# Second cross-attention layer and feed-forward in one stage: a group's feed-forward in 25 steps, one in each half step of later groups' attention

## The chip, the cores and the metric

The kernel runs on one core of a Trainium2 chip. A core has five engines that run beside each other, each with its own instruction stream: TensorE (PE; its weight loads are listed as PEld), VectorE (DVE), ScalarE (ACT), GpSimd (POOL) and SyncE (SP, which here issues nearly all DMA transfers). The metric is device time in microseconds, the median of several runs.

## The reference

The reference is a decoder of two layers over x of 64 sequences x 128 rows x 256 features, each with three pre-normalized parts. The change touches the last two parts of the second layer. Cut to them:

```python
x = x + xattn(layernorm(x), ctx)       # 16 heads of 16 features
x = x + ffn(layernorm(x))

def xattn(y, c):
    q, k, v = (y @ Wq.T + bq) * 0.25, c @ Wk.T + bk, c @ Wv.T + bv     # then split in heads
    return merge_heads(softmax(q @ k.T) @ v) @ Wo.T + bo

def act_quant(x):
    scale = 127.0 / clip(max(abs(x), axis=-1), 1e-5)
    return clip(round(x * scale), -128, 127) / scale

def bit_linear(x, w):                  # weight_quant: ternary weights, one scale
    return act_quant(x) @ weight_quant(w).T

def ffn(x):
    h = bit_linear(x, w1)              # 256 -> 1024
    h = silu(depthwise_conv1d(h, conv_w, 3 taps along the 128 rows) + conv_b)
    return bit_linear(h, w2)           # 1024 -> 256
```

## The kernel before, in words

The work is cut into 16 groups of GB = 4 sequences. The kernel is a row of stages: window attention, cross attention of layer 0 with its slot feed-forward mixed in, causal attention of layer 1 (`stage_attn` with cross False), cross attention of layer 1 (`stage_attn` with cross True), and the feed-forward of layer 1 (`stage_bitnet`). Each stage runs over all groups and hands x on through DRAM: `Flow.reach` loads a group into one of eight SBUF tiles, `Flow.store` and `Flow.flush` write it out (`ab`, `cd`, `de`, `ef`, `out`). The order within an engine is set when the program is built, from the order in which the Python code issues instructions and from estimates of when their inputs are ready; the trace shows such moves, for instance the tap matrices of the last stage (L1156) made on POOL from 2244.6 us, before cross attention began. Waits are put in by the same tool from what each instruction reads and writes.

PSUM has eight banks. Four are the small tiles of `psum(k)` (name `ps`); the other four are one score tile (`sc`) in attention, and four single tiles (`cv`) in the feed-forward.

`attention_stage` works on one sequence at a time in two half steps, for eight heads each. In half step j, `score_burst` (L444) computes scores of sequence j // 2 in the layout that gives a row maximum and, for the sequence one and a half earlier, the transposed scores with the maximum already taken off, 16 and 16 small matmuls into the one score tile. `score_halves` then takes the exponential of the second half on ScalarE (L467; with a bias L464 and L465) and the negated row maximum of the first on VectorE (`negmax`, L471). Even half steps then run `shift_query` (L482, L486) and `divide` (L506 to L513), odd ones `weigh_values` (L494, L499), `turn_output` (L523, L525) and `finish_batch` (L176). At the end of each half step `tick(j)` is called; in `stage_attn` it advances `group_project`, the normalization and projections of the next group (L143, L155, L167, L1046, L1057, L1062, and the addition of the output bias to x on POOL, L1025), which is a generator cut into a few parts.

`stage_bitnet` runs 18 iterations of nine steps, over three groups at once: one group's hidden blocks and convolutions, the scales and rounding of the group before, the output of the one before that. `bitnet_in` normalizes and quantizes x (L1178 to L1192), transposes it (L1198) and spreads the scales over rows (`bcast_rows`, L1166, L1168). `bitnet_hidden` is a bf16 projection (L167) and the scaling into a padded tile `hp` (L1212). `bitnet_conv` does the three taps in one of two ways: for the blocks in `CONV_PE` as three matmuls with diagonal matrices (L1222) and Silu with the bias on ScalarE as eviction (L1226), for the others with one ScalarE step (L1231), two VectorE steps (L1235, L1238) and Silu (L1241). Abs and maxima follow (L1337, L1338), `bitnet_scale` (L1247 to L1268), `bitnet_quant`: the product on POOL (L1276) and rounding on VectorE (L1277), and `bitnet_out` (L1284, L1288).

Of the kernel before, what the change touches and what calls it, by code (L numbers as in the profile page):

```python
# [10 lines left out]
F = mybir.dt.float32  # L11
BF = mybir.dt.bfloat16
# [14 lines left out]
CONV_PE = (0, 1, 3, 4, 6)  # L27
# [978 lines left out]
def stage_attn(k, w, cross, bias=None):  # L1006
    nc = k.nc
    pre = "we" if cross else "wd"
    bias_t, bias_s = bias if bias is not None else (None, None)
    with k.tc.tile_pool(name=pre, bufs=2) as wp, k.tc.tile_pool(name=pre + "1", bufs=1) as w1:  # L1010
        vas = []
        for i in range(2):
            va = w1.tile([S, GB, H, 32], F, name=f"{pre}va{i}")
            nc.gpsimd.memset(va, 0.0)
            nc.gpsimd.memset(va[:, :, :, 16:17], 1.0)
            vas.append(va)
        proj, pending = {}, {}

        def group_project(g):

            xn = w1.tile([S, GB, D], F, tag="xn", name="xn")
            cx = load_group(k, w1, g) if cross else None
# [8 lines left out]
            if cross:  # L1031
                kvT = w1.tile([128, 2, GB * S], F, tag="kvT", name="kvT")
                transpose_group(k, cx, kvT)
            else:
                kvT = xnT
# [3 lines left out]
            for dst, wt, src, sc, bi in (  # L1039
                (qt, w.wq, xnT, w.parq, w.bq), (kt, w.wk, kvT, w.par, w.bk)  # L1040
            ):
                for cc in range(2):
                    p = psum(k)
                    project(k, p, wt, cc * 128, 128, src, 0, GB * S)
                    for par in range(2):
                        nc.scalar.activation(  # L1046
                            dst[:, 2 * cc + par], p, AF.Identity,
                            scale=sc[:, par : par + 1], bias=bi[:, cc, par : par + 1],
                        )
                    yield  # L1050
            va = vas[g % 2]
            for b2 in range(2):
                p = psum(k)
                for j in range(2):
                    b = b2 * 2 + j
                    for kc in range(2):
                        nc.tensor.matmul(  # L1057
                            p[:, j * D : (j + 1) * D], kvT[:, kc, b * S : (b + 1) * S],
                            w.wv[:, kc, :], start=(kc == 0), stop=(kc == 1),
                        )  # L1060
                for j in range(2):
                    nc.vector.tensor_tensor(  # L1062
                        va[:, b2 * 2 + j, :, 0:DH],
                        p[:, j * D : (j + 1) * D].rearrange("p (h d) -> p h d", d=DH),
                        w.bv.rearrange("p (h d) -> p h d", d=DH), ALU.add,
                    )
                if b2 == 0:
                    yield
# [103 lines left out]
def bitnet_in(k, w, g, wp, done):  # L1172
    nc = k.nc
    k.flow.reach(g + 1)
    xn = wp.tile([S, GB, D], F, tag="xn", name="xn")
# [4 lines left out]
    sc = wp.tile([S, GB], F, tag="sc", name="scl")  # L1180
# [10 lines left out]
    xq = wp.tile([S, GB, D], BF, tag="xq", name="xq")  # L1191
# [11 lines left out]
    p = bcast_rows(k, wp, cl, "dg")  # L1203
    isb = wp.tile([128, GB, S], F, tag="isb", name="isb")
    nc.scalar.copy(isb, p.rearrange("p (b l) -> p b l", l=S))
    done.append((xqT, isb))


def bitnet_hidden(k, w, j, xqT, isb, hp):
    p = psum(k)  # L1210
    project(k, p, w.w1, j * 128, 128, xqT, 0, GB * S)
    k.nc.vector.tensor_tensor(  # L1212
        hp[:, :, 1 : S + 1], p.rearrange("p (b l) -> p b l", l=S), isb, ALU.mult
    )


def bitnet_conv(k, w, j, hs, hp):
    nc = k.nc
    if j in CONV_PE:
        pc = k.sc.tile([128, GB, S], F, tag="cv", name="cv")  # L1220
        for t in range(3):
            nc.tensor.matmul(  # L1222
                pc, w.taps[:, CONV_PE.index(j), t, :], hp[:, :, t : t + S],
                start=(t == 0), stop=(t == 2),
            )
        nc.scalar.activation(  # L1226
            hs[:, j, :], pc.rearrange("p b l -> p (b l)"), AF.Silu, bias=w.cb[:, j : j + 1]
        )
        return
    hj = hs[:, j, :].rearrange("p (b l) -> p b l", l=S)  # L1230
    nc.scalar.activation(  # L1231
        hj, hp[:, :, 1 : S + 1], AF.Identity, scale=w.cw[:, j, 1:2],
        bias=w.cb[:, j : j + 1],
    )
    nc.vector.scalar_tensor_tensor(  # L1235
        hj, hp[:, :, 0:S], w.cw[:, j, 0:1], hj, ALU.mult, ALU.add
    )
    nc.vector.scalar_tensor_tensor(  # L1238
        hj, hp[:, :, 2 : S + 2], w.cw[:, j, 2:3], hj, ALU.mult, ALU.add
    )  # L1240
    nc.scalar.activation(hj, hj, AF.Silu)  # L1241


def bitnet_scale(k, w, m4, wp, done):

    nc = k.nc
    nc.vector.tensor_tensor(m4[:, 0:2], m4[:, 0:2], m4[:, 2:4], ALU.max)  # L1247
    mx = wp.tile([128, GB * S], F, tag="mx", name="mx")
    nc.vector.tensor_tensor(mx, m4[:, 0], m4[:, 1], ALU.max)
    p = psum(k)  # L1250
    for b in range(GB):
        nc.tensor.transpose(
            p[:, b * S : (b + 1) * S], mx[:, b * S : (b + 1) * S], k.ident
        )
    yield
    c2 = wp.tile([S, GB], F, tag="c2", name="c2")
# [9 lines left out]
    p = bcast_rows(k, wp, s2, "dg")  # L1266
    s2b = wp.tile([128, GB * S], F, tag="s2b", name="s2b")
    nc.scalar.copy(s2b, p)  # L1268
    done.append((c2, s2b))


def bitnet_quant(k, j, hs, s2b, uq):


    nc = k.nc
    nc.gpsimd.tensor_tensor(hs[:, j], hs[:, j], s2b, ALU.mult)  # L1276
    nc.vector.tensor_scalar(uq[:, j], hs[:, j], MAGIC, MAGIC, ALU.add, ALU.subtract)  # L1277


def bitnet_out(k, w, g, b, uq, c2):  # L1280
    nc = k.nc
    p = psum(k)
    for j in range(8):
        nc.tensor.matmul(  # L1284
            p[:, 0:D], uq[:, j, b * S : (b + 1) * S], w.w2[:, j, :],
            start=(j == 0), stop=(j == 7),
        )
    nc.vector.scalar_tensor_tensor(  # L1288
        k.x[g][:, b, :], p[:, 0:D], c2[:, b : b + 1], k.x[g][:, b, :],
        ALU.mult, ALU.add,  # L1290
    )
    if b == GB - 1:
        k.flow.store(g)


QUANT_AT = {3: (0,), 4: (1, 2), 5: (3,), 6: (4, 5), 7: (6,), 8: (7,)}


def stage_bitnet(k, w):

    nc = k.nc
    with k.tc.tile_pool(name="wf", bufs=2) as wp, k.tc.tile_pool(name="wf1", bufs=1) as w1:
        hps = []
        tap_matrices(k, w, w1)
        for i in range(4):
            hp = w1.tile([128, GB, S + 2], F, name=f"hp{i}")
            nc.gpsimd.memset(hp, 0.0)
            hps.append(hp)  # L1310
        n = 0
        k.flow.reach(0)
        inputs = []
        for _ in bitnet_in(k, w, 0, wp, inputs):
            pass
        scaled = out = None
        for g in range(k.G + 2):
            hs = None
            if g < k.G:
                xqT, isb = inputs.pop()  # L1320
                hs = wp.tile([128, 8, GB * S], F, tag="hs", name="hs")
                m4 = wp.tile([128, 4, GB * S], F, tag="m4", name="m4")
# [195 lines left out]
```

## Time and profile before

| | us |
|---|---|
| median of 3 runs (3495.82 to 3513.59) | 3497.22 |
| the profiled execution | 3494.91 |
| its span, first to last instruction | 3493.1 |
| PE busy in the span | 2893.9 (83%) |
| DVE busy | 2568.4 (74%) |
| ACT busy | 1311.4 (38%) |
| POOL busy | 998.4 (29%) |
| mean granted TensorE clock | 0.910 |

Busy time is the time in which an engine had an instruction running. The span holds all five stages; cross attention of layer 1 begins near 2249 us, with the last matmul of causal attention, and the feed-forward's first matmul starts at 2880.42 us. In rows of groups, the columns are: line, engine, operation, output <- inputs with their shapes, count | busy us, mean ns of one | idle time of the engine just before, and what ended it. The granted clock is a share of TensorE's full speed.

### The profile page before, as it was taken

The page shows a single profiled execution, that of the slowest core. Times are in us where ns is not written, and L with a number is a line of the kernel's source. Part 1 is how long each engine was busy: PE and PEld are TensorE (multiplying, and loading weights), DVE is VectorE, ACT ScalarE, POOL GpSimd, SP SyncE. Part 2 cuts the span into 40 slices and gives each one's busy share as a digit, 9 for nine tenths or more (in the row PEclk, how much of TensorE's full clock was granted, in tenths as well). Part 3 has the DMA queues.
Part 4 walks back from the last instruction along what each step waited for, and adds up shares of the span by engine and source line. Part 5 has one row for each costly group of instructions (what it writes and reads, how often), then busy time and mean ns, then how long its engine had stood idle before and what let it go on. Part 6 is the DMA issues. An engine that isn't in the chain of part 4 may idle for free.

```text
span 3493.1 us, 65076 instructions
## 1 busy us (share of the span) xinstructions
PE 2893.9 (83%) x27764; PEld 1845.9 (53%) x27764; DVE 2568.4 (74%) x4875; ACT 1311.4 (38%) x2012; POOL 998.4 (29%) x920
## 2 busy tenths in 40 slices
PE   5868888588888888878999999699999977777776
PEld 2433333366666666645666666466766753333332
DVE  6867786566666666658989889766665559888876
ACT  1121111144444444424444444244445534444442
POOL 6446555343333433220000000210010003334323
PEclk9869999699999999979999999899999998888887
DMA  4100100101011010000000000101111110001000
GB/s 143 61 13 25 37 31 31 49 14 38 20 37 38 19 38 26 13 37 13 26 26 25 26 26 26 49 32 38 38 56 38 48 40 12 24 24 37 13 13 24
DMA packets 59249, 115.20 MB, mean 33 GB/s; under 512 B 6496, under 2 KB 39664, under 8 KB 58704
## 3 DMA queue, kind: packets, MB, share of 16 engines
q1 hardware_dynamic: 58304, 109.29, 8.9%
q8 instruction: 219, 3.59, 0.4%
q0 software_dynamic: 656, 1.75, 0.2%
q14 instruction: 70, 0.57, 0.1%
HBM read 69.08 MB, written 41.94 MB: 32 GB/s over the span
## 4 chain that ended last, share of the span: by engine, by line
PE 41%; DVE 37%; POOL 9%; ACT 7%; issue 4%; DMA 1%; SPq 0%; POOLq 0%; DVEq 0%; ACTq 0%
PE sc L444 10%; PE ps L167 7%; DVE negmax L471 6%; PE ps L176 5%; PE ps L494 4%; DVE uq L1277 4%; DVE sb L458 3%; DVE e L464 3%; PE cv L1222 2%; DVE xn L143 2%; DVE pv L350 2%; ACT e L465 2%; DVE oT L354 2%; PE ps L482 2%; PE ps L1057 2%
## 5 line engine op out<-in xcount | busy, mean ns | idle before, releaser
L444 PE MATMUL sc<-kt,qt 32*128 32x128 f32 x6144 | 517.7, 296 | 150.8 <-DVE negmax L471 93.0
L444 PEld LDWEIGHTS sc<-kt,qt 32*128 32x128 f32 x6144 | 422.9, 195 | 330.0 <-issue 151.0
L444 PE MATMUL sc<-q,kt 32*128 32x128 f32 x6144 | 490.6, 295 | 5.6 <-DVE q L486 3.0
L471 DVE TENSOR_REDUCE negmax<-sc 128x8 f32<-128x1024 f32 x256 | 312.4, 1220 | 159.7 <-ACT e L467 154.5
L444 PEld LDWEIGHTS sc<-q,kt 32*128 32x128 f32 x6144 | 406.3, 195 | 25.7 <-DVE rec L509 11.4
L467 ACT ACTIVATE e<-sc 128x1024 f32<-128x1024 f32 x256 | 261.5, 1021 | 296.8 <-PE sc L444 296.5
L1222 PE MATMUL cv<-hp,taps 128*128 128x512 f32 x480 | 263.3, 692 | 60.5 <-DVE hp L1212 59.8
L292 POOL TENSOR_TENSOR pr<-pad,qt 128x896 f32<-128x896 f32 x128 | 244.9, 1947 | 188.9 <-ACT pad L279 180.8
L486 DVE TENSOR_TENSOR q<-ps,qt 128x512 f32<-128x512 f32 x192 | 131.7, 686 | 154.3 <-PE ps L482 154.3
L1276 POOL TENSOR_TENSOR hs<-hs,s2b 128x512 f32<-128x512 f32 x128 | 177.2, 1418 | 194.7 <-ACT s2b L1268 194.7
L465 ACT ACTIVATE e<-e 128x1024 f32<-128x1024 f32 x128 | 135.3, 1057 | 241.7 <-DVE e L464 241.7
L458 DVE TENSOR_TENSOR sb<-sc,bias_s 128x1024 f32<-128x1024 f32 x128 | 156.2, 1220 | 69.4 <-PE sc L444 69.4
L1222 PEld LDWEIGHTS cv<-hp,taps 128*128 128x128 f32 x480 | 98.2, 215 | 192.3 <-issue 95.0
L350 DVE TENSOR_TENSOR pv<-sc,pad 128x896 f32<-128x896 f32 x128 | 136.9, 1082 | 73.4 <-PE sc L344 73.3
L136 POOL TENSOR_TENSOR ln_rs<-ln_ve,expo 128x4 f32<-128x4 f32 x96 | 101.2, 1054 | 304.0 <-DVE ln_ve L135 166.4
L1025 POOL TENSOR_TENSOR x<-x,t_d_bo 128x1024 f32<-128x1024 f32 x16 | 37.6, 2351 | 490.5 <-DVE xn L143 490.5
L499 ACT COPY avs<-ps 128x512 f32<-128x512 f32 x192 | 112.2, 584 | 149.1 <-PE ps L494 149.1
L1025 POOL TENSOR_TENSOR x<-x,t_e_bo 128x1024 f32<-128x1024 f32 x16 | 37.5, 2344 | 443.1 <-DVE xn L143 443.1
L464 DVE TENSOR_TENSOR e<-sc,bias_t 128x1024 f32<-128x1024 f32 x128 | 155.4, 1214 | 1.6 <-PE sc L444 1.3
L471 DVE TENSOR_REDUCE negmax<-sb 128x8 f32<-128x1024 f32 x128 | 154.8, 1210 | 0.0
L133 DVE BATCH_NORM_STATS2 ln_st<-x 128x6 f32<-128x256 f32 x384 | 152.2, 426 | 2.6 <-DMA x<-cd 0.6
L1277 DVE TENSOR_SCALAR uq<-hs 128x512 bf16<-128x512 f32 x128 | 146.4, 1191 | 7.3 <-POOL hs L1276 7.3
(329 smaller groups left out, 6450.4 us busy)
## 6 DMA issues: line engine op xcount, KB each, us to landing
cx<-in_ctx_dram SPq DMA_DIRECT2D x32, 512.0 KB, 4.1
x<-in_x_dram SPq DMA_DIRECT2D x16, 512.0 KB, 3.9
ab<-x SPq DMA_DIRECT2D x16, 512.0 KB, 2.6
x<-ab SPq DMA_DIRECT2D x16, 512.0 KB, 3.2
cd<-x SPq DMA_DIRECT2D x16, 512.0 KB, 2.6
x<-cd SPq DMA_DIRECT2D x16, 512.0 KB, 3.2
de<-x SPq DMA_DIRECT2D x16, 512.0 KB, 2.6
x<-de SPq DMA_DIRECT2D x16, 512.0 KB, 3.2
```

The source lines that it names most:

```text
L167: k.nc.tensor.matmul(out, w[:, kc, c0 : c0 + cn], rhsT[:, kc, n0 : n0 + n], start=(kc == 0), stop=(kc == 1),)
L292: k.nc.gpsimd.tensor_tensor(pr[:, c], shift_windows(t.kt, b, c), t.qt[:, c, b, :].unsqueeze(1).to_broadcast([128, WIN, S]), ALU.mult,)
L350: nc.vector.tensor_tensor(pv, bc[th][:, :, 0 : WIN * 64].rearrange("p c (l w) -> p c l w", w=WIN), shift_windows2(t.vt, b, th), ALU.mult,)
L444: k.nc.tensor.matmul(t[:, side * 2 + rr, c * S : (c + 1) * S], st[rows, c, :], mv[rows, c, :], start=True, stop=True,)
L458: nc.vector.tensor_tensor(sb, src, bias_s[:, hf * 2 : hf * 2 + 2, :], ALU.add)
L464: nc.vector.tensor_tensor(e, t[:, 2:4, :], bias_t[:, hf * 2 : hf * 2 + 2, :], ALU.add)
L465: nc.scalar.activation(e, e, AF.Exp)
L467: nc.scalar.activation(e, t[:, 2:4, :], AF.Exp)
L471: nc.vector.tensor_reduce(b.lay.extra(b.nm, hf * 2), src.rearrange("p r (c m) -> p r c m", m=S), AX.X, ALU.max, negate=True,)
L1222: nc.tensor.matmul(pc, w.taps[:, CONV_PE.index(j), t, :], hp[:, :, t : t + S], start=(t == 0), stop=(t == 2),)
L1276: nc.gpsimd.tensor_tensor(hs[:, j], hs[:, j], s2b, ALU.mult)
L1277: nc.vector.tensor_scalar(uq[:, j], hs[:, j], MAGIC, MAGIC, ALU.add, ALU.subtract)
```

## The change

Cross attention and feed-forward of layer 1 become one stage, `stage_last`. x is loaded from `de` and stored to `out`; `ef` is gone, with its 16 stores and 16 loads of 512 KB.

The feed-forward of a group is a generator, `bitnet_group`, with 24 yields and so 25 steps: normalization and scaling; the rounding to bf16; transposes and scales; eleven steps of hidden blocks and convolutions; the scale of the hidden layer in two; four steps of products and rounding; four of output; and the end. `tick(j)` starts group g's at half step 8g + 15, just after the last sequence of that group is finished, and group g's projections at 8g - 7; then it advances everything that runs by one step. So up to three groups' feed-forwards are on their way beside the attention of the later groups, and after the last half step of attention (137) `tick` goes on alone to 160.

Further differences: the convolution's matmuls write a small tile (`ps`) instead of `cv`; block set `CONV_PE` has four blocks instead of five; Silu is no longer part of the eviction but is done for two pairs of blocks at a time, together with Abs, in inner steps 5 and 9, and the maxima follow one step later; Abs has one buffer (`AB_BUFS`); `hp` has three tiles instead of four; the hidden layer is held as pairs of blocks in six buffers; values are held in three tiles of two sequences instead of two of four; the context tile `cx` is loaded one group ahead. `stage_attn` is split: `stage_causal` is its other half, with the same work, and `project_heads` and `project_values` hold the common parts.

```diff
-CONV_PE = (0, 1, 3, 4, 6)
+CONV_PE = (0, 2, 4, 6)
+AB_BUFS = 1
...
+def bitnet_conv(k, w, j, y, hp):
+    nc = k.nc
+    if j in CONV_PE:
+        p = psum(k)
+        pc = p.rearrange("p (b l) -> p b l", l=S)
+        for t in range(3):
+            nc.tensor.matmul(
+                pc, w.taps[:, CONV_PE.index(j), t, :], hp[:, :, t : t + S],
+                start=(t == 0), stop=(t == 2),
+            )
+        nc.scalar.activation(y, p, AF.Identity, bias=w.cb[:, j : j + 1])
+        return
+    yj = y.rearrange("p (b l) -> p b l", l=S)
+    nc.scalar.activation(
+        yj, hp[:, :, 1 : S + 1], AF.Identity, scale=w.cw[:, j, 1:2],
+        bias=w.cb[:, j : j + 1],
+    )
+    for t in (0, 2):
+        nc.vector.scalar_tensor_tensor(
+            yj, hp[:, :, t : t + S], w.cw[:, j, t : t + 1], yj, ALU.mult, ALU.add
+        )
+def bitnet_group(k, w, g, wp, w1, hps):
+    nc = k.nc
+    xn = w1.tile([S, GB, D], F, tag="xn", name="xn")
     layernorm(k, wp, g, xn)
...
         xn, xn, MAGIC + 127.0, MAGIC - 128.0, ALU.min, ALU.max
     )
+    yield
+    xq = w1.tile([S, GB, D], BF, tag="xq", name="xq")
     nc.vector.tensor_scalar(xq, xn, MAGIC, None, ALU.subtract)
     yield
...
+    yield
+    pairs = []
+    m = w1.tile([128, GB * S], F, tag="m", name="m")
+    maxima = []
+    for j in range(11):
+        if j in (0, 2, 4, 6):
+            pairs.append(wp.tile([128, 2, GB * S], F, tag="hs", name="hs", bufs=6))
+        if j < 8:
+            bitnet_hidden(k, w, j, xqT, isb, hps[(8 * g + j) % len(hps)])
+        if 0 < j < 9:
+            bitnet_conv(
+                k, w, j - 1, pairs[(j - 1) // 2][:, (j - 1) % 2], hps[(8 * g + j - 1) % len(hps)]
+            )
+        for i, ab in maxima:
+            if i == 0:
+                nc.vector.tensor_tensor(m, ab[:, 0], ab[:, 1], ALU.max)
+            else:
+                nc.vector.tensor_tensor(ab[:, 0], ab[:, 0], ab[:, 1], ALU.max)
+                nc.vector.tensor_tensor(m, m, ab[:, 0], ALU.max)
+        maxima = []
+        if j in (5, 9):
+            two = (0, 1) if j == 5 else (2, 3)
+            for i in two:
+                nc.scalar.activation(pairs[i], pairs[i], AF.Silu)
+            for i in two:
+                ab = w1.tile([128, 2, GB * S], F, tag="ab", name="ab", bufs=AB_BUFS)
+                nc.scalar.activation(ab, pairs[i], AF.Abs)
+                maxima.append((i, ab))
+        yield
...
+    uq = w1.tile([128, 8, GB * S], BF, tag="uq", name="uq")
+    for i in range(4):
+        for j in range(2):
+            hs = pairs[i][:, j]
+            nc.gpsimd.tensor_tensor(hs, hs, s2b, ALU.mult)
+            nc.vector.tensor_scalar(uq[:, 2 * i + j], hs, MAGIC, MAGIC, ALU.add, ALU.subtract)
+        yield
+    for b in range(GB):
+        p = psum(k)
+        for j in range(8):
+            nc.tensor.matmul(
+                p[:, 0:D], uq[:, j, b * S : (b + 1) * S], w.w2[:, j, :],
+                start=(j == 0), stop=(j == 7),
+            )
+        nc.vector.scalar_tensor_tensor(
+            k.x[g][:, b, :], p[:, 0:D], c2[:, b : b + 1], k.x[g][:, b, :],
+            ALU.mult, ALU.add,
+        )
+        if b == GB - 1:
+            k.flow.store(g)
+        yield
+def stage_last(k, w, wf):
+    nc = k.nc
+    with k.tc.tile_pool(name="we", bufs=2) as wp, k.tc.tile_pool(name="we1", bufs=1) as w1:
+        vas = []
+        for i in range(3):
+            va = w1.tile([S, 2, H, 32], F, name=f"weva{i}")
+            nc.gpsimd.memset(va, 0.0)
+            nc.gpsimd.memset(va[:, :, :, 16:17], 1.0)
+            vas.append(va)
+        tap_matrices(k, wf, w1)
         hps = []
+        for i in range(3):
             hp = w1.tile([128, GB, S + 2], F, name=f"hp{i}")
             nc.gpsimd.memset(hp, 0.0)
             hps.append(hp)
+        qts, kts, cxs = {}, {}, {}
+        def group_project(g):
+            xn = w1.tile([S, GB, D], F, tag="xn", name="xn")
+            layernorm(k, wp, g, xn)
+            nc.gpsimd.tensor_tensor(
+                k.x[g], k.x[g], w.bo.unsqueeze(1).to_broadcast([S, GB, D]), ALU.add
+            )
+            yield
+            xnT = w1.tile([128, 2, GB * S], F, tag="xnT", name="xnT")
+            transpose_group(k, xn, xnT)
+            kvT = w1.tile([128, 2, GB * S], F, tag="kvT", name="kvT")
+            transpose_group(k, cxs.pop(g), kvT)
+            yield
+            qts[g] = wp.tile([128, 4, GB * S], F, tag="qt", name="qt")
+            for cc in range(2):
+                project_heads(k, qts[g], w.wq, cc, xnT, w.parq, w.bq)
+                if cc == 0 and g + 1 < k.G:
+                    cxs[g + 1] = load_group(k, w1, g + 1)
+                    k.flow.reach(g + 1)
+                yield
+            kts[g] = wp.tile([128, 4, GB * S], F, tag="kt", name="kt")
+            for cc in range(2):
+                project_heads(k, kts[g], w.wk, cc, kvT, w.par, w.bk)
+                yield
+            for b2 in range(2):
+                project_values(k, w, vas[(2 * g + b2) % 3], kvT, b2)
+                yield
+        def prep(bi):
+            g, b = divmod(bi, GB)
+            t = Batch()
+            t.qt, t.kt = qts[g][:, :, b * S : (b + 1) * S], kts[g][:, :, b * S : (b + 1) * S]
+            t.va, t.row_scale = vas[(bi // 2) % 3][:, b % 2], None
+            xb = k.x[g][:, b, :]
+            def fin(y):
+                nc.vector.tensor_tensor(xb, y, xb, ALU.add)
+            t.fin = fin
+            return t
+        running = []
+        def tick(j):
+            if j % 8 == 7 and 0 <= j // 8 - 1 < k.G:
+                running.append(bitnet_group(k, wf, j // 8 - 1, wp, w1, hps))
+            if j % 8 == 1 and (j + 7) // 8 < k.G:
+                running.append(group_project((j + 7) // 8))
+            running[:] = [q for q in running if next(q, q) is not q]
         k.flow.reach(0)
+        cxs[0] = load_group(k, w1, 0)
+        for j in range(-7, 0):
+            tick(j)
+        attention_stage(k, wp, w1, prep, w.wo, Heads(True), tick=tick)
+        j = 2 * k.NB + 10
+        while running:
+            tick(j)
+            j += 1
...
-        ab, cd, de, ef = (between(k, n) for n in ("ab", "cd", "de", "ef"))
+        ab, cd, de = (between(k, n) for n in ("ab", "cd", "de"))
...
-                stage_attn(k, p.d, False, p.bias)
-        Flow(k, de, ef)
+                stage_causal(k, p.d, p.bias)
+        Flow(k, de, outside(k, "out"))
         with scores("scE", 1) as k.sc:
-            stage_attn(k, we, True)
-        Flow(k, ef, outside(k, "out"))
-        with scores("scF", 4) as k.sc:
-            stage_bitnet(k, p.f)
+            stage_last(k, we, p.f)
```

## The prediction

> **What bounds the kernel now.** I read the busy time by stretch first. Columns: stretch, its length, then busy us (x instructions) of PE, PEld, DVE, ACT and POOL, the granted TensorE clock, DMA share, GB/s.
>
> ```profile
> core 0: us, PE busy (x) PEld busy (x) DVE busy (x) ACT busy (x) POOL busy (x), PEclk, DMA share, GB/s
> 1700.00:1800.00 100.00, 91.63 (x1138) 64.18 (x1141) 89.97 (x134) 43.18 (x60) 6.74 (x4) 0.97 0.06 23
> 2255.00:2870.00 615.00, 562.80 (x7808) 419.12 (x7808) 374.61 (x683) 289.99 (x416) 59.02 (x39) 0.98 0.12 42
> 2343.00:2860.00 517.00, 480.23 (x6880) 359.85 (x6879) 311.26 (x550) 249.84 (x360) 38.27 (x22) 0.99 0.13 44
> 2870.00:3493.00 623.00, 455.41 (x1504) 213.69 (x1504) 510.16 (x949) 253.31 (x417) 215.02 (x160) 0.83 0.06 22
> ```
>
> The two stages that the change joins are the third and fifth lines. Cross attention (from 2249 us) is bound by TensorE, 93% busy in its steady part, with VectorE at 60%. The feed-forward is bound by VectorE, 82% busy over the stage, with TensorE at 73% and a clock of only 0.83. So each has room on the engine that the other fills. The second line is causal attention: there both engines run at 90% and 92% beside each other, so such a balance can be reached with four small PSUM tiles and one score tile, which is what the joined stage has too.
>
> Next the groups of the feed-forward, kept apart by shape, and the spread of one of them:
>
> ```profile
> L1222 PE MATMUL cv<-hp,taps 128*128 128x512 f32 x480 | 263.3, 692 | 60.5 <-DVE hp L1212 59.8
> L1276 POOL TENSOR_TENSOR hs<-hs,s2b 128x512 f32<-128x512 f32 x128 | 177.2, 1418 | 194.7 <-ACT s2b L1268 194.7
> L1277 DVE TENSOR_SCALAR uq<-hs 128x512 bf16<-128x512 f32 x128 | 146.4, 1191 | 7.3 <-POOL hs L1276 7.3
> L1212 DVE TENSOR_TENSOR hp<-ps,isb 128x512 f32<-128x512 f32 x128 | 86.8, 682 | 30.3 <-PE ps L167 30.1
> ...
> L1277 DVE TENSOR_SCALAR uq<-hs x128: 409/1483/1504, 2920.2 to 3485.3; 128x512 bf16<-128x512 f32 x128
> ```
>
> A rounding (L1277) takes 409 ns alone and some 1480 ns beside a POOL product (L1276, 1418 ns): it waits until that one ends. Last the timeline of the convolution twice, and the waits of the attention stage (us in total, times, longest):
>
> ```profile
> 3157.37 5.42 PE L1222 MATMUL cv<-hp,taps 128*128 128x512 f32 x6 [2.49 <-DVE hp L1212]
> 3164.01 2.84 PE L1222 MATMUL cv<-hp,taps 128*128 128x512 f32 x6 [0.78 <-DVE hp L1212]
> ...
> DVE negmax L471 <- ACT e L467: 96.9, 61, 2.6
> PEld sc L444 <- DVE negmax L471: 63.1, 47, 4.3
> ```
>
> The same six matmuls take 5.42 us after TensorE stood still for VectorE, and 2.84 us a little later: part of the feed-forward's TensorE time is a low clock. The last two lines show the loop that stays: a score burst waits until the one score tile has been read by negmax.
>
> **The change part by part.** Cross attention runs in half steps. Negmax (L471) goes 128 times, from 2276.7 to 2851.8 us: 575.1/127 = 4.53 us each. The feed-forward's output stores go from 2961.6 to 3489.0 us: 527.4/15 = 35.2 us a group, 4.40 us for an eighth. One after the other that is 8.93 us; from the end of the causal stage's matmuls (2249 us) to the end it is 1244 us.
>
> *VectorE in a joined half step.* Attention: 311.3/517 x 4.53 = 2.73 us. Feed-forward: 510.2/128 = 3.98. Convolution blocks on TensorE go from five to four of eight, so 16 blocks gain two VectorE steps (L1235, L1238, 775 and 744 ns): 24 us, 0.19 a half step. Sum 6.90. POOL's products may run ahead of the roundings, for they need only s2b; then roundings take less than 1191 ns. With half of them alone at 409 ns that is 64 x 0.78 = 50 us less than at most 100 us, about 0.3 a half step net of what other VectorE steps lose beside POOL: 6.6 to 6.9.
>
> *TensorE.* Attention: 480.2/517 x 4.53 = 4.21. Feed-forward: 455.4 less some 10 of attention's end, at clock 0.83; at 0.98, 377. A fifth of L1222 goes: 263/5 x 0.83/0.98 = 45. So 332, 2.6 a half step; sum 6.8. If the clock stayed at 0.83 for the feed-forward's part it would be 7.2; I take 0.98, since TensorE no longer stands idle for long.
>
> *ScalarE.* Silu leaves the convolution's eviction and is done on pairs. Before: 54.6 + 38.8 + 30.2 + 67.4 = 191 us (L1226, L1231, L1241, L1337). After: 64 x 0.683 + 64 x 0.808 + 64 x 1.06 + 64 x 1.054 = 231, 40 more. New are table switches: Silu now comes twice a group between exponentials, 4 loads a group, 64 in all. The trace has such loads in the slot stage:
>
> ```profile
> 1003.24 1.28 ACT L467 ACT_TABLE_LOAD   x1 [0.49 <-PE sc L444]
> 1004.53 1.02 ACT L467 ACTIVATE e<-sc 128x1024 f32<-128x1024 f32 x1
> ```
>
> The next exponential begins as the load ends, so I count 1.28 us each, 82 us; ScalarE has 290 + 253 + 40 + 82 = 665 us. The Trainium skill, "ScalarE: Activation LUTs", section "What ACT_TABLE_LOAD costs", speaks against the change more: a load and then a drain of about 1380 ns, 2.66 us for every switch, 170 us in all. What counts is the burst: two Silu, two Abs, two loads, 4 x 1.055 + 2 x 1.28 = 6.8 us, beside 3.5 us of other ScalarE work in that half step: 10.3 us, 2.6 above a half step of 7.7. If nothing absorbs it, 32 bursts cost 83 us by the row; by the page 5.4 us each, 170. I take the row, and nearly nothing of it (0.1 a half step), since TensorE and VectorE have other work and four PSUM tiles of lead.
>
> *New waits.* Abs has one buffer, so the second of two waits for VectorE's maximum of the first; an exponential queued behind on ScalarE would then hold the score tile, and the next burst. The convolution now takes one of the four small PSUM tiles instead of its own four; TensorE waits when VectorE or ScalarE is late with an eviction, and scores queue behind. With some six tiles a half step and four to hold, each may live 5 us. The bound from below is nothing; from above it is the round trip in the slow rival. Hidden behind the full engines: value tiles and hp (three instead of four) are reused a half step or more after their last reader.
>
> *Queues.* SP loses 16 stores and 16 loads of 512 KB (ef; 2.9 and 3.2 us to landing, DMA share 0.12): off the path. cx comes one group earlier (4.1 us to landing, eight half steps of cover); uncovered it would cost 4.1 us a group. Loads of x wait for stores eight half steps older. The stores of out lie on the path only once, for the last group, as before. POOL has 59 + 215 us: the bias addition (2344 ns) and the products share one queue; ln_rs behind one of them is late by 1.4 us, with VectorE's normalization behind it, covered by other VectorE work.
>
> *Sum.* Both engines need 6.6 to 6.9 us; at causal attention's 89 to 90% that is 7.4 to 7.75. With the table loads I take 7.7 us.
> - head, from 2249 us to the first score burst at 2276: 27 us, unchanged
> - half steps 0 to 14, attention alone: 15 x 4.53 = 68
> - half steps 15 to 127, both: 113 x 7.7 = 870
> - half steps 128 to 137, without new scores or projections: VectorE 2.73 less negmax 1.22 less projections 0.9, plus 4.17, at 89%: 5.4, so 55
> - the end: group 15 is at its fourth step. Eight inner steps at 3.0 us (the spacing at the start of the feed-forward now), 5 for Silu and Abs, and from the last convolution to the end 32 as now (3461 to 3493): 60
>
> Sum 1080 against 1244: 164 us less. The span 3493.1 becomes 3329, the profiled execution's 3494.9 becomes 3331; the median shown is 2.3 above that execution, so 3333.
>
> **The rivals.**
> 1. *Better overlap.* Roundings mostly alone and both engines at 95%: 7.1 us, 802 us for the middle, 232 saved: 3265. For it: 93% in cross attention now. Against: two engines near full at once showed 90 to 92%.
> 2. *ScalarE's bursts are not absorbed.* The 83 us come on top: 3416; with the page's drain 170 us, which leaves nothing of the gain. For it: negmax already waits 96.9 us for the exponential's turn. Against: ScalarE has four tenths free.
> 3. *Slower: one score tile makes a round trip of it.* A burst needs negmax of the burst before, and negmax queues behind a step's feed-forward work on VectorE. If VectorE idles through each burst (16 pairs, 1.16 us), stalls as often as in the feed-forward alone (15% idle, 0.7 us) and bursts of ScalarE add 83/113 = 0.7, a half step is 6.9 + 1.2 + 0.7 + 0.7 = 9.5: 1074 for the middle, 40 us lost, 3537. It decides from (1244 - 210)/113 = 9.15 us. For it: the waits of 63.1 us above. Against: causal attention has the same tile and VectorE at 90%.
> 4. *The steps don't mix.* If the order on the engines left the feed-forward behind attention, only the gap between the stages would go (2867 to 2880, TensorE idle): 3482.
>
> **How the numbers follow.** Likeliest 0.60; better 0.13; bursts 0.16; slower 0.09; not mixed 0.02. The range reaches from a little under the better case to beyond the bursts, up to 8.9 us a half step: 3240 to 3470. A measurement of this kernel tells about 0.5% from no change, 17 us. Faster 0.87, same 0.03, slower 0.10.
>
> **What would show it.** Right: negmax 7 to 8.3 us apart over most of one stage; both engines at 85% or more there; clock 0.95 or higher; about 64 more table loads; no ef; roundings below 1191 ns on average. Wrong: ScalarE's wait lines at Silu and Abs with TensorE idle behind them; negmax 9 us apart; table loads well above 64; more than 100 us from the last score to the end.

## The result, and the profile after

The kernel after takes 3544.19 us (median; 3542.84 to 3555.68) against 3496.52 us of the kernel before, measured beside it: ratio 1.0133, 95% interval 1.0095 to 1.0171. It is slower by 48 us where 164 less was predicted. The span is 3543.0 us.

First the busy time by stretch again (stretch, length, then PE, PEld, DVE, ACT, POOL busy with instructions, TensorE clock, DMA share, GB/s), for the joined stage:

```profile
2350.00:2450.00 100.00, 83.10 (x859) 55.25 (x871) 65.71 (x135) 64.72 (x85) 9.31 (x6) 0.93 0.04 12
2550.00:2650.00 100.00, 72.53 (x689) 49.31 (x700) 77.86 (x149) 55.68 (x75) 24.48 (x18) 0.88 0.05 17
2950.00:3050.00 100.00, 76.60 (x705) 50.88 (x715) 77.82 (x147) 55.68 (x75) 23.50 (x16) 0.89 0.05 17
```

In the last two rows nothing is full: TensorE is busy 73 to 77%, VectorE 78%, ScalarE 56%. The work was put side by side, but all engines wait. Negmax (L472) comes 128 times. From the seventeenth, at 2351.2 us, to the last, at 3420.7, 111 half steps take 9.64 us each on average, and in the steady part a group of eight takes 78.6 to 80.2 us, mostly 78.7, with nearly the same pattern every time: 6.8, 10.5, 4.9, 12.3, 3.6, 13.2, 14.0 and 13.5 us from one negmax to the next. So there is no uniformly slow half step; a few long ones make the sum.

The groups and the spread that answer to those of before, with the table loads (line, engine, operation, tiles, count | busy us, mean ns | idle before, and what ended it):

```profile
L1293 POOL TENSOR_TENSOR hs<-hs,s2b 128x512 f32<-128x512 f32 x128 | 184.8, 1477 | 675.0 <-ACT s2b L1285 675.0
L1294 DVE TENSOR_SCALAR uq<-hs 128x512 bf16<-128x512 f32 x128 | 143.1, 1173 | 5.1 <-POOL hs L1293 5.1
L1264 ACT ACT_TABLE_LOAD x56 | 71.8, 1283 | 68.5 <-DVE scl L1215 56.2 <-DVE hs L1201 6.6 <-DVE cl L1213 5.0
L468 ACT ACT_TABLE_LOAD x55 | 70.6, 1283 | 1.0
L1259 DVE TENSOR_TENSOR m<-m,ab 128x512 f32<-128x512 f32 x48 | 71.8, 1495 | 0.5
...
L1294 DVE TENSOR_SCALAR uq<-hs x128: 398/1481/1502, 2463.4 to 3535.7; 128x512 bf16<-128x512 f32 x128
```

The roundings got almost no relief (1173 ns instead of 1191). The maximum of two SBUF tiles, L1259, is long as well, 1495 ns on average; it takes 687 in tie_dve, below. There are 111 loads in the stage, not 64. The waits from 2450 to 3250 us (us in total, times, longest):

```profile
PEld sc L445 <- DVE negmax L472: 101.6, 37, 6.3
DVE negmax L472 <- ACT e L468: 96.6, 50, 3.2
ACT L1264 <- DVE scl L1215: 51.1, 10, 5.1
```

In 800 us TensorE's weight loads stood 101.6 us before a score burst for negmax, and negmax itself 96.6 us for the exponential. Why, is seen in the chain of waits of one group (start, us, what), over the intervals of 14.0 and 13.5 us:

```profile
2934.69 1.03 ACT e L468
2935.74 1.23 DVE negmax L472
2936.97 0.59 DVE hp L1177
2937.56 1.47 DVE ab L1258
2939.03 5.65 DVE uq L1294 x4
2944.68 1.67 DVE m L1259
2946.35 3.48 DVE uq L1294 x4
2949.83 1.13 DVE negmax L472
...
2957.76 0.66 DVE hs L1201
2958.41 0.10 DVE scl L1215
2958.51 1.26 ACT L1264
2959.78 1.06 ACT hs L1264
2960.86 1.28 ACT L468
2962.15 1.03 ACT e L468
2963.21 1.23 DVE negmax L472
```

Two things are to be seen. The code spreads a group's eight roundings over four half steps; the built order has all eight between two negmaxes, most of them stretched beside POOL's products: 9.13 us of 14.1. Two of the maxima (`ab`, `m`) stand with them and take 1.47 and 1.67 us. And ScalarE stands at a Silu that waits for L1201 (the profile of after names `scl`, the step just behind it); the exponential, whose scores have long been there, comes behind it and behind two loads. The same is so in three more of the eight intervals, the second, fourth and sixth: each has a Silu between two loads ahead of its exponential. These became theory B (the roundings) and theory A (Silu, loads and Abs ahead of the exponential). The rival, theory C, was that one score tile makes a round trip whatever stands in between.

### The profile page after: what moved, and what is told of

Same layout as the page of the kernel before. It is cut to its first block, busy times and chain, and to the rows that moved or that the text cites. A ratio compares the mean times of both kernels' runs of the same rounds, so it can differ in the third digit from the quotient of the medians.

```text
span 3543.0 us, 64882 instructions
## 1 busy us (share of the span) xinstructions
PE 2869.4 (81%) x27554; PEld 1874.5 (53%) x27668; DVE 2607.7 (74%) x4923; ACT 1482.9 (42%) x2138; POOL 1004.8 (28%) x918
## 4 chain that ended last, share of the span: by engine, by line
DVE 38%; PE 34%; ACT 15%; POOL 8%; issue 3%; DMA 1%; SPq 0%; POOLq 0%; DVEq 0%; ACTq 0%
PE sc L445 8%; DVE negmax L472 6%; PE ps L177 5%; PE ps L168 5%; PE ps L495 4%; DVE uq L1294 4%; DVE sb L459 3%; DVE e L465 3%; ACT e L468 2%; PE ps L1189 2%; DVE xn L144 2%; DVE pv L351 2%; ACT L1264 2%; DVE oT L355 2%; POOL ln_rs L137 2%
## 5 line engine op out<-in xcount | busy, mean ns | idle before, releaser
L445 PE MATMUL sc<-kt,qt 32*128 32x128 f32 x6144 | 537.2, 304 | 216.4 <-DVE negmax L472 158.6
L445 PEld LDWEIGHTS sc<-kt,qt 32*128 32x128 f32 x6144 | 440.2, 203 | 397.5 <-DVE negmax L472 215.0
L445 PE MATMUL sc<-q,kt 32*128 32x128 f32 x6144 | 511.5, 304 | 13.7 <-DVE negmax L472 8.8
L472 DVE TENSOR_REDUCE negmax<-sc 128x8 f32<-128x1024 f32 x256 | 312.6, 1221 | 198.9 <-ACT e L468 192.2
L445 PEld LDWEIGHTS sc<-q,kt 32*128 32x128 f32 x6144 | 425.4, 204 | 35.0 <-DVE negmax L472 10.0
L1293 POOL TENSOR_TENSOR hs<-hs,s2b 128x512 f32<-128x512 f32 x128 | 184.8, 1477 | 675.0 <-ACT s2b L1285 675.0
L1189 PE MATMUL ps<-hp,taps 128*128 128x512 f32 x384 | 179.9, 605 | 23.3 <-DVE hp L1177 20.4
L1196 ACT ACTIVATE hs<-hp,t_g_cb,g_cws 128x512 f32<-128x512 f32 x64 | 52.0, 813 | 290.1 <-DVE hp L1177 236.4
L472 DVE TENSOR_REDUCE negmax<-sb 128x8 f32<-128x1024 f32 x128 | 154.9, 1210 | 0.0
L1294 DVE TENSOR_SCALAR uq<-hs 128x512 bf16<-128x512 f32 x128 | 143.1, 1173 | 5.1 <-POOL hs L1293 5.1
L345 PE MATMUL sc<-fw,spread 32*128 32x448 f32 x512 | 110.7, 656 | 36.9 <-DVE pv L351 22.2
```

The costliest lines, as they stand in the source:

```text
L445: k.nc.tensor.matmul(t[:, side * 2 + rr, c * S : (c + 1) * S], st[rows, c, :], mv[rows, c, :], start=True, stop=True,)
L472: nc.vector.tensor_reduce(b.lay.extra(b.nm, hf * 2), src.rearrange("p r (c m) -> p r c m", m=S), AX.X, ALU.max, negate=True,)
L1189: nc.tensor.matmul(pc, w.taps[:, CONV_PE.index(j), t, :], hp[:, :, t : t + S], start=(t == 0), stop=(t == 2),)
L1293: nc.gpsimd.tensor_tensor(hs, hs, s2b, ALU.mult)
L1294: nc.vector.tensor_scalar(uq[:, 2 * i + j], hs, MAGIC, MAGIC, ALU.add, ALU.subtract)
```

## The experiments

Times are medians in us; each ratio is to the kernel before in the same series, whose medians lay from 3496.5 to 3508.3. Differences below are of medians; between two series they are uncertain by up to these 12 us. A group is taken in the steady part.

| kernel | us | ratio, 95% interval | a group, us |
|---|---|---|---|
| after | 3544.2 | 1.0133 (1.0095 to 1.0171) | 78.6 to 80.2 |
| no_switch | 3446.1 | 0.9828 (0.9801 to 0.9854) | 71.6 |
| no_product | 3398.5 | 0.9703 (0.9675 to 0.9731) | 70 |
| no_both | 3362.6 | 0.9599 (0.9571 to 0.9628) | 68 |
| pin_round | 3497.1 | 0.9987 (0.9973 to 1.0000) | 74.1 to 77.5 |
| pace | 3502.5 | 0.9989 (0.9970 to 1.0007) | 75.2 |
| two_tiles | 3481.2 | 0.9926 (0.9900 to 0.9952) | 73.7 |
| tie | 3401.2 | 0.9702 (0.9669 to 0.9735) | 68.3 |
| pace_tie_late | 3445.4 | 0.9822 (0.9792 to 0.9852) | 71.7 |
| tie_two | 3408.5 | 0.9711 (0.9674 to 0.9749) | 68.6 to 70.6 |
| dve | 3452.3 | 0.9838 (0.9802 to 0.9874) | 73 |
| tie_dve | 3313.1 | 0.9434 (0.9386 to 0.9482) | 63.1 |
| tie_dve_pin | 3371.8 | 0.9613 (0.9577 to 0.9650) | 68.3 |
| tie_tanh | 3382.8 | 0.9647 (0.9630 to 0.9664) | 66.1 to 68.1 |

In several edits `behind(k, x)` stands for placing an instruction in the built order behind x, on the same engine.

**Which cost is there at all.** Leave out the table switches, the products, or both.

```diff
 no_switch:
-                nc.scalar.activation(pairs[i], pairs[i], AF.Silu)
+                nc.scalar.activation(pairs[i], pairs[i], AF.Tanh)
 no_product:
-            nc.gpsimd.tensor_tensor(hs, hs, s2b, ALU.mult)
```

> The joined stage with Tanh in place of Silu, so the hidden layer's function is another one; Tanh and Exp share a table, so the 111 table loads of the joined stage (1.283 us each, 142 us of ScalarE) go. Theory A (ScalarE: loads, Silu and Abs stand before exponentials, and the exponential holds the score tile): 90 to 140 us less than the changed kernel, 3405 to 3455 us, and the waits of score bursts shrink. Theory B (VectorE: roundings held up by POOL's products stand before negmax): less than 30 us, 3515 or more. Theory C (one score tile makes a round trip whatever the other engines do): less than 30 us here and in the next two runs.

> The joined stage without POOL's products of the hidden layer with its scales (the product is left out, the rounding stays): roundings take 409 ns instead of 1173. Theory B: the eight roundings of a group between two negmaxes take 3.3 instead of 11 us, so some 7 to 8 us a group, 100 to 125 us in all: 3420 to 3445. Theory A: less than 30 us, since the roundings lie beside ScalarE's bursts: 3515 or more. Theory C: less than 30 us.

> Both of these leave-outs together. If A and B each hold for their own part of the 79 us period and the parts add up: 200 to 260 us less, 3285 to 3345 us, the half step that the sums of engine time allow (7.1 to 7.7 us). If they hide each other: about as the better of the two. Theory C: above 3480.

98 us went with the switches, 146 with the products (more than theory B's 100 to 125), 182 with both (less than the 200 to 260 of two parts that add up). In no_product the mean rounding is 418 ns, the maxima L1258 and L1259 take 90.6 us in place of 117.3, and of the eight intervals only the one of 14.0 us moves much, to 5.3. So A and B are both real, with an overlap of 98 + 146 - 182 = 62 us, and C alone doesn't explain the time. But no_both, with both costs absent, still needs 8.5 us a half step: these runs take work away, and show no place where it hurts.

**Spreading the roundings by order.** The whole computation; each rounding behind the negmax of its half step.

```diff
-            nc.vector.tensor_scalar(uq[:, 2 * i + j], hs, MAGIC, MAGIC, ALU.add, ALU.subtract)
+            with behind(k, k.negmax):
+                nc.vector.tensor_scalar(uq[:, 2 * i + j], hs, MAGIC, MAGIC, ALU.add, ALU.subtract)
```

> The whole computation; each pair of roundings is tied, in issue order alone, behind the negmax of the half step whose tick issues it, so that the build can no longer place all eight between two negmaxes. Theory B, where it is the place: 6 to 7 us a group, 85 to 110 us less than the changed kernel, 3435 to 3460. Theory B, where it is the lock and not the place: roundings still some 1170 ns and less than 30 us gained. Theory A: less than 30 us.

The mean rounding fell to 640 ns, but the kernel by 47 us and not by 85 to 110: the lump came back elsewhere. From the timeline of pin_round (start, us, engine, line):

```profile
2996.03 11.20 POOL L1293 TENSOR_TENSOR hs<-hs,s2b 128x512 f32<-128x512 f32 x8 [46.86 <-ACT s2b L1285]
...
3007.19 2.14 POOL L137 TENSOR_TENSOR ln_rs<-ln_ve,expo 128x4 f32<-128x4 f32 x2
3008.24 1.38 DVE L144 TENSOR_SCALAR xn<-x,ln_mv,ln_rs 128x256 f32<-128x256 f32 x4 [3.37 <-POOL ln_rs L137]
...
3012.88 1.28 ACT L1264 ACT_TABLE_LOAD   x1 [8.39 <-DVE scl L1215]
```

POOL's eight products now stand in its queue ahead of ln_rs; the normalization waits for that, L1201 behind it, Silu for L1201, and the exponential behind Silu: one interval of 18.3 us. The next kernel puts the products behind ln_rs as well, and a new group's steps first in `tick`.

```diff
+            with behind(k, k.rs):                    # k.rs: the last ln_rs
                 nc.gpsimd.tensor_tensor(hs, hs, s2b, ALU.mult)
...
-                running.append(bitnet_group(k, wf, j // 8 - 1, wp, w1, hps))
+                running.insert(0, bitnet_group(k, wf, j // 8 - 1, wp, w1, hps))
```

> The whole computation. As in pin_round a rounding is issued behind the negmax of its half step; in addition POOL's products are issued behind the last ln_rs, and a new group's steps come first in their tick. Theory B (the eight products and roundings of a group stand in one lump, first before a negmax, in pin_round before ln_rs): the 18.3 us interval of pin_round falls to 10 to 13 us, a group takes 72 to 76 us instead of 77, and the kernel 3430 to 3470 us, that is 30 to 65 less than pin_round. Rival (the lump only moves on, to the next step that stands behind POOL): within 15 of pin_round, 3482 to 3512, with another interval of over 16 us.

The rival was right: 3502 us, and an interval of 19.4 us. With ln_rs out of the way it is the normalization itself that now stands beside the products: 56 of its steps take some 1.36 us, each beside a product, and the mean is 829 ns. Durations in pace, then of the same step in tie_dve (below), min/median/max ns:

```profile
L149 DVE TENSOR_SCALAR xn<-x,ln_mv,ln_rs x125: 396/409/1366, 2248.7 to 3405.2; 128x256 f32<-128x256 f32 x125
```

```profile
L149 DVE TENSOR_SCALAR xn<-x,ln_mv,ln_rs x128: 402/408/415, 2265.8 to 3251.0; 128x256 f32<-128x256 f32 x128
```

**ScalarE's queue.** Silus in one piece behind the last exponential, and the next exponential behind them.

```diff
+            with behind(k, k.silu):
-            nc.scalar.activation(e, t[:, 2:4, :], AF.Exp)
+                k.exp = nc.scalar.activation(e, t[:, 2:4, :], AF.Exp)
...
+                with behind(k, k.exp if i == two[0] else k.silu):
-                nc.scalar.activation(pairs[i], pairs[i], AF.Silu)
+                    k.silu = nc.scalar.activation(pairs[i], pairs[i], AF.Silu)
```

> The whole computation. The two Silus of a burst are issued one right behind the other and behind the last exponential, and the next exponential behind them, so that a group needs 4 loads of a table, not 7: 55 loads in the joined stage instead of 111, 56 x 1.283 = 72 us less on ScalarE. Theory A (loads before exponentials hold the score tile): of the 98 us that went with all loads about half go, 40 to 60 us less than the kernel after, 3485 to 3505. Rival (it is the length of the whole burst, two Silus, Abs and loads in one piece, that holds the exponential, and tying makes it longer in one place): within 20 us of the kernel after, 3525 to 3565.

143 us less, far more than the 40 to 60 expected, and more than the 72 us by which ScalarE's loads shrank (55 left in the stage). The waits of tie from 2450 to 3250 us:

```profile
PEld sc L450 <- DVE negmax L478: 99.2, 23, 8.0
...
DVE negmax L478 <- ACT e L474: 45.1, 22, 2.6
```

Negmax waits for the exponential 45.1 us instead of 96.6. Where, the eight intervals of a group tell: 4.7, 5.4, 5.5, 11.4, 3.9, 9.4, 13.6 and 14.5 us. Silus stand in two of them now, the fourth and the seventh, instead of four. The second and the sixth, which lost theirs, are 5.1 and 3.8 us shorter. The last one, of the chain above, is no shorter (14.5 against 13.5): ScalarE no longer stands at a Silu there, but at another step of the feed-forward, with the exponential behind it as before. And theory B's lump is untouched: the seventh takes 13.6 us, the burst waits up to 8.0 us for negmax, and the mean rounding is 1299 ns. Whether the loads' length or the place on the queue was the cost, tie_tanh was to tell.

```diff
 tie_tanh, from tie:
-                    k.silu = nc.scalar.activation(pairs[i], pairs[i], AF.Silu)
+                    k.silu = nc.scalar.activation(pairs[i], pairs[i], AF.Tanh)
```

> tie with another function in place of Silu (tanh, which needs no switch), so that the joined stage has no load of a table; ScalarE's order is tie's, apart from what the build moves for itself. The output is another function's. tie took away 56 loads and also moved the Silus behind the exponential that was ready; this leaves the place and takes the other 55 loads, 70.6 us of ScalarE. If loads cost by their length wherever they stand: 50 to 70 us less than tie, 3330 to 3350. If it was the place in the queue (an exponential behind a Silu that itself waits): within 20 of tie, 3380 to 3421, and no_switch (3446) with no load at all but the old place stays above it.

Taking the remaining 70.6 us of loads away gives 18 us, just within the 20 us of the second forecast (the kernel before had the same median in both series). The place alone, from no_switch to tie_tanh, with no load in the stage on either side, gives 63 us. It isn't the wait for VectorE at the head of a burst that went: a step of the burst stands as long for `scl` in both, with the exponential behind it (ScalarE's waits from 2450 to 3250 us, no_switch, then tie_tanh):

```profile
ACT hs L1264 <- DVE scl L1215: 61.5, 12, 5.1
ACT ab L1274 <- DVE scl L1222: 69.5, 12, 5.8
```

What went is the Silu and the Abs ahead of the exponential in the second and the sixth interval. So a load in such a place costs little; what costs, by these two intervals, is the number of half steps in which long work of the feed-forward stands ahead of the exponential. The edit both pairs the Silus and puts them behind an exponential; what each of the two gives was not run apart.

**The score tile.** Two tiles of two banks in the last stage.

```diff
+    if k.split:
+        t = [k.sc.tile([128, 2, 512], F, tag=f"sc{i}", name=f"sc{i}") for i in range(2)]
...
-                    t[:, side * 2 + rr, c * S : (c + 1) * S], st[rows, c, :], mv[rows, c, :],
+                    t[side][:, rr, c * S : (c + 1) * S], st[rows, c, :], mv[rows, c, :],
```

> The whole computation. In the last stage the score tile is two tiles of two banks, one that negmax reads and one that the exponential reads; before, both halves were one tile, so that negmax waited for the exponential by order of the tile, and the next burst for both. Theory A/C (the late exponential holds negmax, and the round trip of the one tile is the period): the 108 us in which negmax waited for the exponential go, and a part of the 120 of the bursts: 40 to 100 us less than the kernel after, 3445 to 3505. Rival (a burst fills both halves in turn, so it waits for the later of the two readers anyway, and the lumps on VectorE and ScalarE stay): less than 20, 3525 to 3560.

> The whole computation. tie with the score tile as two tiles of two banks. two_tiles alone gave 63 us, tie 143. If both took the same waits (an exponential that is late holds negmax): within 20 of tie, 3381 to 3421. If two_tiles takes its own, the burst that waits for both readers: 30 to 60 less, 3340 to 3370.

63 us alone: negmax no longer waits for the exponential. On top of tie there is nothing, 3408.5 against 3401.2 us, as forecast for two edits that take the same waits. One score tile is thus no bound by itself: it passes a late reader on. Two tiles on top of tie_dve, below, were not run.

**Both ties together.**

```diff
 pace_tie_late: pace and tie, and
-    for j in range(11):
+    for j in range(12):
...
-        if j in (5, 9):
-            two = (0, 1) if j == 5 else (2, 3)
+        if j in (6, 10):
+            two = (0, 1) if j == 6 else (2, 3)
```

> The whole computation. Both edits (pace and tie), and each pair of Silus one inner step later, 6 and 10 of twelve, so that its last input is older. Theories A and B together: 3370 to 3430 us, faster than both kernels, with a group at 69 to 72 us; the gains add as 98 and 146 did in part (182). Rival (what is saved in one wait comes back in the next): 3450 or more.

A miss: 44 us slower than tie alone. Spreading by order brought a lump elsewhere for the third time (one interval of 18.8 us). The later Silus are a third change in this kernel, and were not run alone.

**Taking the cause of the lump away.** The products on VectorE, so that they hold up nothing from POOL.

```diff
-            nc.gpsimd.tensor_tensor(hs, hs, s2b, ALU.mult)
+            nc.vector.tensor_tensor(hs, hs, s2b, ALU.mult)
```

> The whole computation. The 128 products of hidden layer and scale are done on VectorE, not on POOL. VectorE's own sum hardly moves: a product like hp (682 ns) and a rounding alone (418 ns in no_product) are 1.10 us against 1.17 of the waiting rounding, 8.8 us a group against 8.9. What goes is all that stands behind POOL's products: ln_rs on POOL's queue, and the normalization xn (L144), which took 5.18 us beside products and 1.38 without. Theory B, read as a lock (POOL's products hold several steps of VectorE): 40 to 80 us less than the kernel after, 3465 to 3505. Rival (it is the lump of eight VectorE steps ahead of one negmax, whatever makes them long; it stays): within 20 of the kernel after, 3525 to 3565.

> The whole computation. tie with the products on VectorE, in the build's own order, so that the eight of a group still stand close together. From tie's 3401: lock 20 to 60 less, 3340 to 3380; lump within 15, 3386 to 3416.

> The whole computation. As tie_dve, with each product and rounding issued behind the negmax of its half step: two pairs, 2.2 us, in each of four half steps, in place of 8.8 us ahead of one. If the lump counts: the intervals of 13 to 14 us that tie still has go, a group comes from 68.3 us to 64 to 66, and the kernel is 30 to 65 less than tie: 3336 to 3371. If the sums of the engines bound it by now (VectorE 81% and TensorE 87% busy in tie): within 20 of tie_dve.

dve takes 92 us less than after, more than the 40 to 80 forecast, though VectorE does more: products and roundings take it 83.7 + 50.3 = 134 us instead of 143.1. The maxima L1258 and L1259, which stood beside the products, gain as well, 87.9 us instead of 117.3 (what stays long there stands beside POOL's addition of the output bias). That makes 38 us of VectorE's time; the rest of the 92 is put down to the places. From the timeline of dve, between two negmaxes:

```profile
2967.19 1.23 DVE L472 TENSOR_REDUCE negmax<-sc 128x8 f32<-128x1024 f32 x1 [2.72 <-ACT e L468]
...
2968.92 1.29 DVE L1293 TENSOR_TENSOR hs<-hs,s2b 128x512 f32<-128x512 f32 x2
...
2970.12 0.76 DVE L1294 TENSOR_SCALAR uq<-hs 128x512 bf16<-128x512 f32 x2
2970.80 1.29 DVE L1293 TENSOR_TENSOR hs<-hs,s2b 128x512 f32<-128x512 f32 x2
2972.00 0.76 DVE L1294 TENSOR_SCALAR uq<-hs 128x512 bf16<-128x512 f32 x2
...
2974.48 1.22 DVE L472 TENSOR_REDUCE negmax<-sc 128x8 f32<-128x1024 f32 x1
```

Only about half of the group's steps now stand ahead of this negmax; the interval is 7.3 us instead of 14.0, and it is the only one of the eight that is much shorter. That the build places them better because their durations are now what it assumes is argued, not shown.

With both edits tie_dve takes 3313.1 us, 5.7% less than before and below what either side had forecast (3340 to 3380, or 3386 to 3416), and the gains add up: 4.3 points of the ratio from tie, 3.0 from dve, 7.0 together. The stretches and waits of tie_dve:

```profile
2650.00:2850.00 200.00, 184.75 (x1845) 120.39 (x1844) 167.76 (x368) 128.64 (x181) 18.38 (x14) 0.97 0.08 25
2850.00:3050.00 200.00, 185.38 (x1804) 120.53 (x1802) 167.09 (x368) 127.37 (x178) 19.34 (x13) 0.97 0.07 22
...
PEld sc L450 <- DVE negmax L478: 52.1, 37, 3.4
DVE negmax L478 <- ACT e L474: 49.0, 26, 2.6
```

TensorE is 92% busy at clock 0.97, with VectorE at 84%; the burst's wait for negmax is half of after's. That is what the prediction had described, reached by another order of the same computation and with the products on another engine. It also beats no_both (3362.6 us), which does less work: the places were worth more than the work.

tie_dve_pin fits neither side: its time is at the upper end of what the lump forecast, but a group takes 68.3 us, not 64 to 66, and it is 59 us slower than tie_dve although its roundings lie two and two in four half steps. One interval grew from 6.0 to 11.0 us; in it VectorE meets POOL's addition of the output bias:

```profile
2954.26 2.36 POOL L1342 TENSOR_TENSOR x<-x,t_e_bo 128x1024 f32<-128x1024 f32 x1 [10.58 <-DVE xn L149]
...
2954.46 2.71 DVE L1207 SCALAR_TENSOR_TENSOR hs<-hp,g_cws,hs 128x512 f32<-128x512 f32 x1
```

The step L1207 takes 2.71 us instead of 0.75; in tie_dve none of its 128 takes over 0.753. That explains 2 of the 5 us; what the other steps that moved cost was not run apart.

## Why the prediction was wrong

- **The half step of 7.7 us.** This is the step that failed: "at causal attention's 89 to 90% that is 7.4 to 7.75". 9.64 us were measured. The sum of the work was nearly right; that the queues would let both engines be that busy was not. 111 half steps x (9.64 - 7.7) = 215 us, which is the whole miss (164 + 48 = 212). In tie_dve the same 111 half steps, from 2351.0 to 3206.1 us, take 7.70 each. So 7.7 is within this stage's reach, but not in the built order of after. That the figure is met to the hundredth is luck: TensorE's part was larger than predicted and its share higher, 92% and not 90 (below). Causal attention's balance was taken over to a stage whose queues hold long pieces ahead of negmax and the exponential: eight roundings in a row, a Silu between two loads.
- **The table loads**, "nearly nothing of it": 64 were counted from the code, 111 came, since the build put an exponential between the two Silus of a burst. Leaving them out gave 98 us. The bound of the bursts (83 us) was near in size by luck: it counted two bursts a group of 10.3 us each, where Silus stood ahead of the exponential in four half steps; gathered in two they cost 143 us less (tie), and there the loads are worth only 18 (tie_tanh). The row of 1.283 us a load held; the added drain of the Trainium skill, "ScalarE: Activation LUTs", section "What ACT_TABLE_LOAD costs", is not seen here: in the chain above the Silu begins 0.01 us after its load.
- **The roundings**, "POOL's products may run ahead": they could not, for s2b comes just before (POOL idle for 46.99 us in one group of after, then eight products without a gap), and the eight roundings stood in one place. The prediction had the mean of 1191 ns on its desk and counted it as VectorE's work, with a relief of 0.3 us a half step; what the products hold up in one place, the roundings and two of the maxima, was worth 146 us when the products were left out, and 92 when they were moved.
- **TensorE**, 6.8 us a half step: in tie_dve 0.92 x 7.9 = 7.3 at clock 0.97, in after 0.77 x 9.84 = 7.6 at 0.90. The term was too small by about 0.5: the score matmul's mean went from 285 to 293 ns in tie_dve and 308 in after, and the feed-forward's part was scaled fully with the clock. For the scores the clock alone would make 291 and 313 ns of 285 (an estimate, from 0.99 before to 0.97 and 0.90), so it explains most of theirs. The convolution's matmul, 692 ns before at 0.83, takes 635 in tie_dve, where full scaling with the clock would make it 592. What else makes up the 0.5 is open. VectorE's sum held: 0.83 x 7.9 = 6.6 in tie_dve.
- **Head and end** held: the first 16 half steps end at 2351 us as attention alone would, and from the last negmax to the end it is 122 us against 115.
- **Rival 3** has the time (3537), by luck, and the place, a burst that waits for negmax, but not its parts: the loss isn't 9.5 us in each half step by a round trip; it sits in the long intervals of a group, and in tie_dve the one tile does not prevent 7.70. Its argument against, causal attention's 90% with the same tile, was true and proved nothing about this stage.
- **Signs.** All four signs of being wrong came: ScalarE's wait at Silu with TensorE idle behind, negmax over 9 us apart, loads well above 64, and 106 us from the last score to the end. Of the signs of being right, roundings below 1191 ns came too, at 1173; that tells nothing.

## What to carry to other kernels

When two stages are laid over each other, sum the engines, but then ask for each queue what the longest piece is that can stand ahead of the short instruction on which the other stage's loop turns (here negmax and the exponential), and in how many turns of the loop it does. A count taken from the code (four loads, two roundings a half step) is a hope until the built order confirms it. Where a lump comes from a conflict between engines, take the conflict away: three attempts to spread it by order moved it to another place and gained 47 us at most, and moving the product to the busier VectorE gained 92 us.

## What the runs showed of the hardware

Beside POOL's work not only the rounding is stretched (398 ns alone, 1481 ns median in after): the normalization with two scalar operands went from 409 to 1366 ns in pace, and a step with two SBUF inputs, L1207, from 0.75 to 2.71 us beside an addition of 2.36 in tie_dve_pin. POOL loses too: that addition took 2353 ns at the median in tie_dve_pin and 2723 in after. The Trainium skill, "SBUF — State Buffer", section "SBUF: two separate sides", describes a pair of ports that VectorE and GpSimd share and that whichever starts first holds for its whole instruction. The durations agree: the 2.71 us of L1207 begin 0.20 us into the addition and end 0.55 us after it. And a table load took 1.283 us and no more, with the next instruction 0.01 us behind it.
